# Four graph layers on one core: all start times of a planned instruction order laid out anew

## The chip, the cores and the metric

One core of one Trainium2 chip. The metric is the device time of one execution in microseconds (us), 64 graphs long.

## The reference, cut to what matters

64 graphs of 256 nodes with 512 features, float32. Each of four layers normalises the rows, applies relu, computes a graph layer and adds it to its input.

```python
def reference(x, adj, nodemask, ...):            # x 64x256x512, adj 64x256x256
    h = jnp.maximum(_layernorm(x, axis=-1), 0.0)
    x = x + _L0_gnn_ref(h, adj, ...)   # one softmax weight per node, times the values h @ Wv
    h = jnp.maximum(_layernorm(x, axis=-1), 0.0)
    x = x + _L1_gnn_ref(h, adj, ...)   # 8 heads of additive attention, masked by adj
    h = jnp.maximum(_layernorm(x, axis=-1), 0.0)
    x = x + _L2_gnn_ref(h, adj, ...)   # 8 heads, tanh(adj * scores)
    h = jnp.maximum(_layernorm(x, axis=-1), 0.0)
    x = x + _L3_gnn_ref(h, adj, nodemask, ...)   # as layer 0 with an adjacency aggregate
    return x
```

## The kernel before

A graph is some 150 named steps, each of which issues a few instructions on one engine. A table gives every step a time; the steps of all graphs are sorted by `graph * PERIOD + time`, and that sorted list is the order on each engine. No step waits for its time: the program takes only the order from the tables (a graph took 58.22 us in the trace that the prediction used, where `PERIOD` is 59.0). So the numbers of the tables are an order and nothing else. Some four to five graphs are in flight at once (by the plan 282.6 / 59).

```python
PERIOD = 59.0
TIMES = {
    "load": 0.000, "st0": 8.598, "at": 14.291, "rs0": 17.770, "pw0": 18.151, "sh0": 19.827, "hn0": 20.197,
    # ... some 140 more steps ...
    "softp3": 265.594, "pv31": 265.839, "softv3": 268.089, "softa3": 268.742, "pv30": 269.380, "softw3": 274.098,
    "add3": 280.909, "store": 282.605,
}
# ... WEIGHTS: the same for the set-up; FIRST: own tables of the first graphs; LAST: of the last ones ...

    def sequence(count):
        steps = [(at, -1, name) for name, at in WEIGHTS.items()]
        for b in range(count):
            times = FIRST[b] if b < len(FIRST) else LAST[b - count] if count - b <= len(LAST) else TIMES
            steps += [(b * PERIOD + at, b, name) for name, at in times.items()]
        return sorted(steps)
```

The steps that the argument touches, for a layer n: statistics `st`, variance plus epsilon `rs`, the power on GpSimd `pw`, the shift `sh`, relu on ScalarE `hn`, the 32x32 turn `sq`, the write of the turned squares to a scratch in DRAM `sw`, and the four reads that bring them back fully turned, `ht`. All transfers are issued through SyncE's queue (each line of the page's DMA issues is SPq), in the order of the sorted list.

```python
        @step("load")
        def _():
            nc.sync.dma_start(g.take("xt"), x[b].rearrange("(p c) d -> p c d", c=NC))           # 512 KB
            nc.sync.dma_start(g.take("adj", 4), adj[b].rearrange("(p c) m -> p c m", c=NC))     # 256 KB
            blocks = g.take("blocks")
            for q in range(4):                                                                  # 256 KB
                nc.sync.dma_start(blocks[q * S:(q + 1) * S],
                                  adj[b].rearrange("(a i) (q e) -> q i a e", i=S, q=4)[q])
# ...
            @step(f"pw{layer}")
            def _():
                nc.gpsimd.tensor_tensor(st["rstd"], st["rstd"], power, OP.pow)

            @step(f"sh{layer}")
            def _():
                st["shift"] = small.tile([P, NC], F32, name="shift")
                nc.vector.scalar_tensor_tensor(st["shift"], st["mv"][:, :, 0], -1.0, st["rstd"],
                                               op0=OP.mult, op1=OP.mult)
# ...
            @step(f"sw{layer}")
            def _():
                out_by_squares()               # one dma_start, 512 KB to the scratch

            @step(f"ht{layer}")
            def _():
                gathered(g.take("ht", users), st["sq_d"])   # four dma_start of 128 KB
```

TensorE steps: `qk`, `score0`, `pv` (values), `fa`/`fb` (features of layer 1), `po` and `su` (attention outputs and row sums), `xp` (projection), `xc` (C product), `ps`, `py` (layer 2 scores and outputs), `agg0`, `z` (layer 3).

## Time and profile before

| | |
|---|---|
| time, median of 3 runs | 3922.32 us (3916.96 to 3927.03) |
| medians of the rounds on the five chips used below | 3901 to 3916 us |
| TensorE busy | 94% of the span |
| span of the profiled execution the prediction used | 3892.8 us |

The profiled execution took 3894.62 us (its span, from the first to the last instruction, is 3892.8). The lines of the profile are in the prediction. There, the fences show in turn the page's busy times and slices, two windows, and the timelines of TensorE, VectorE and GpSimd.

### The profile page before, as it was taken

The numbers are of one execution on the slowest core, as the hardware profiler recorded it, in microseconds if no ns is written. First come the engines' busy times: TensorE is split into PE (matmuls) and PEld (weight loads), VectorE is DVE, ScalarE is ACT, GpSimd is POOL, SyncE is SP. The second block draws the span as 40 slices with busy tenths as digits, with TensorE's granted clock in tenths as the row PEclk, the third lists the DMA queues.
The fourth block names the chain that finished last, engine by engine and source line by source line (L and its number), as shares of the span: only waits on it lengthen the run. The fifth ranks groups of instructions, "written<-read, shape, count | busy, mean of one in ns | idle before, by whom it ended". The sixth has DMA issues, their size and how long they took to land.

```text
span 3892.8 us, 52870 instructions
## 1 busy us (share of the span) xinstructions
PE 3677.6 (94%) x16322; PEld 2126.0 (55%) x16322; DVE 3060.4 (79%) x7449; ACT 1872.2 (48%) x3653; POOL 1531.4 (39%) x1229
## 2 busy tenths in 40 slices
PE   6789999999999999999999999999999999999889
PEld 3455555555555555555555555555555555555544
DVE  5777787887888787787787787887788787787784
ACT  2444554545545544545544544545545544544442
POOL 1434343444344344343344344343344344344341
PEclk9899999999999999999999999999999999999999
DMA  7565666666666666666666666666666666666553
GB/s 200 168 193 179 208 200 212 214 203 213 216 201 211 217 200 212 207 199 207 215 195 213 207 202 214 214 204 209 216 201 216 214 198 215 209 200 196 181 182 103
DMA packets 967435, 784.71 MB, mean 202 GB/s; under 512 B 788913, under 2 KB 859121, under 8 KB 942577
## 3 DMA queue, kind: packets, MB, share of 16 engines
q1 hardware_dynamic: 967152, 781.34, 63.8%
q8 instruction: 130, 2.13, 0.2%
q14 instruction: 153, 1.25, 0.1%
HBM read 511.12 MB, written 270.01 MB: 201 GB/s over the span
## 4 chain that ended last, share of the span: by engine, by line
PE 46%; DVE 20%; DMA 17%; SPq 8%; issue 5%; POOL 3%; ACT 2%; DVEq 0%; ACTq 0%; POOLq 0%
PE bank L639 34%; DVE sq L645 7%; DMA ht<-sq_d 6%; SPq L650 5%; DMA sq_d<-sq 5%; PE bank L1111 4%; PE bank L966 3%; DVE pair L948 2%; DVE junk L896 2%; DMA hn<-sq_d 2%; PE bank L1097 2%; DVE stats L690 2%; DMA blocks<-in_adj_dram 2%; DVE xt L775 2%; DVE shift L706 1%
## 5 line engine op out<-in xcount | busy, mean ns | idle before, releaser
L639 PE MATMUL bank<-w_s,ht 128*128 128x256 f32 (+2 forms) x3072 | 965.7, 462 | 80.7 <-DMA ht<-sq_d 69.0
L639 PE MATMUL bank<-wv_s,ht 128*128 128x512 f32 x2048 | 906.3, 594 | 0.0
L639 PEld LDWEIGHTS bank<-w_s,ht 128*128 128x128 f32 x3072 | 587.4, 198 | 381.3 <-issue 288.2
L713 ACT ACTIVATE hn<-xt,shift,rstd 128x512 f32<-128x512 f32 x512 | 388.7, 806 | 828.8 <-DVE shift L706 759.5
L942 POOL TENSOR_TENSOR pair<-pair,negt 128x1024 f32<-128x1024 f32 x256 | 604.5, 2374 | 117.2 <-ACT pair L935 117.2
L639 PEld LDWEIGHTS bank<-wv_s,ht 128*128 128x128 f32 x2048 | 397.3, 197 | 444.8 <-issue 442.8
L975 POOL TENSOR_TENSOR half<-pair 128x512 f32<-128x512 f32 x256 | 331.3, 1306 | 593.1 <-PE bank L989 328.0
L896 DVE CUSTOM_DVE_ANT_0 junk<-all,adj 128x256 f32<-128x256 f32 x1024 | 472.8, 462 | 31.4 <-issue 0.2
L639 PE MATMUL bank<-m_s,ht 128*128 128x512 f32 x1024 | 455.5, 597 | 8.2 <-DMA ht<-sq_d 6.8
L935 ACT ACTIVATE pair<-all,ec 128x256 f32<-128x256 f32 x1024 | 433.4, 497 | 9.8 <-DMA all<-er_d 9.8
L1149 POOL TENSOR_TENSOR xt<-xt,hn 128x512 f32<-128x512 f32 x64 | 111.4, 1741 | 811.7 <-DMA hn<-sq_d 811.7
L690 DVE BATCH_NORM_STATS2 stats<-xt 128x6 f32<-128x512 f32 x512 | 332.3, 680 | 96.3 <-POOL xt L1034 88.5
L701 POOL TENSOR_TENSOR rstd<-rstd,power 128x2 f32<-128x2 f32 x256 | 179.5, 702 | 407.0 <-DVE rstd L697 390.9
L645 DVE STREAM_TRANSPOSE sq<-hn 128x512 f32<-128x512 f32 x512 | 331.8, 686 | 5.0 <-ACT hn L713 4.9
L966 PE MATMUL bank<-pair,feats 128*64 128x256 f32 x2048 | 272.4, 401 | 62.2 <-ACT pair L954 62.0
L1129 DVE TENSOR_TENSOR pair<-bank,at 128x512 f32<-128x512 f32 x512 | 317.0, 669 | 12.2 <-PE bank L1097 12.0
L954 ACT ACTIVATE pair<-pair 128x1024 f32<-128x1024 f32 x256 | 264.0, 1050 | 118.4 <-DVE pair L948 111.2
L639 PEld LDWEIGHTS bank<-m_s,ht 128*128 128x128 f32 x1024 | 197.2, 198 | 221.4 <-issue 216.4
L948 DVE TENSOR_TENSOR pair<-pair,all 128x1024 f32<-128x1024 f32 x256 | 303.4, 1223 | 15.3 <-DMA all<-m_d 14.4
L1032 POOL TENSOR_TENSOR hn<-hn,rs 128x256 f32<-128x256 f32 x256 | 152.3, 617 | 392.4 <-DMA hn<-sq_d 317.7
L761 ACT ACTIVATE bank<-bank,nmax 128x256 f32<-128x256 f32 x128 | 56.8, 443 | 504.5 <-DVE nmax L756 504.5
L1136 ACT ACTIVATE pair<-pair 128x512 f32<-128x512 f32 x512 | 285.8, 617 | 16.1 <-DVE pair L1129 16.0
(83 smaller groups left out, 4541.8 us busy)
## 6 DMA issues: line engine op xcount, KB each, us to landing
sq_d<-sq SPq DMA_DIRECT2D x448, 512.0 KB
ht<-sq_d SPq DMA_DIRECT2D x1024, 128.0 KB
all<-er_d SPq DMA_DIRECT2D x128, 1024.0 KB
all<-m_d SPq DMA_DIRECT2D x64, 1024.0 KB
hn<-sq_d SPq DMA_DIRECT2D x512, 128.0 KB
xt<-in_x_dram SPq DMA_DIRECT2D x64, 512.0 KB
xpt<-sq_d SPq DMA_DIRECT2D x256, 128.0 KB
out_dram<-xt SPq DMA_DIRECT2D x64, 512.0 KB
```

The lines of the kernel that those rows point to most:

```text
L639: nc.tensor.matmul(p, chunk(ht[:, k], c), w[:, k], start=(k == 0), stop=(k == KC - 1))
L645: nc.vector.transpose(sq.rearrange("p (r k i c) -> p c k r i", r=4, k=KC, c=NC)[:, c], t[:, c])
L690: nc.vector.bn_stats(stats[:, c, :], g["xt"][:, c, :])
L713: nc.scalar.activation(hn[:, c, :], g["xt"][:, c, :], AF.Relu, bias=st["shift"][:, c:c + 1], scale=st["rstd"][:, c:c + 1])
L896: nc.vector.tensor_tensor_reduce(junk, g["en"][:, h, :], g["adj"][:, c, :], 1.0, -BIG, OP.add, OP.max, g["mx"][:, c, h:h + 1])
L935: nc.scalar.activation(e[:, s, j, :], g["es"][:, h, :], AF.Prelu, bias=st["ec"][:, j, H + h:H + h + 1], alpha=0.2)
L942: nc.gpsimd.tensor_tensor(e, e, g["negt"][:, None].to_broadcast([P, 2, NC, N]), OP.add)
L948: nc.vector.tensor_tensor(e, e, g["m"][:, 2 * p:2 * p + 2, None, :].to_broadcast([P, 2, NC, N]), OP.subtract)
L966: nc.tensor.matmul(po[s * U:(s + 1) * U, p % 2, :], feats[:, j, h * U:(h + 1) * U], e[:, s, j, :], start=(j == 0), stop=(j == NC - 1))
L975: nc.gpsimd.tensor_tensor(g.take("half", name=f"h{p}"), e[:, :, 0, :], e[:, :, 1, :], OP.add)
L1129: nc.vector.tensor_tensor(th[:, s], g[f"ps{p}{s}"].rearrange("p (m n) -> p m n", m=NC), g["at"], OP.mult)
L1136: nc.scalar.activation(g[f"th{p}"][:, s], g[f"th{p}"][:, s], AF.Tanh)
```

## The change

Intent: a new plan with a shorter period (57 in place of 59) and no slack beyond the durations that a trace had shown. The instructions stay the same; every table (`TIMES`, `WEIGHTS`, six `FIRST` graphs, five `LAST` graphs) is replaced. The only other edit gives some set-up banks distinct names.

```diff
-PERIOD = 59.0
+PERIOD = 57.0
 TIMES = {
-    "load": 0.000, "st0": 8.598, "at": 14.291, "rs0": 17.770, "pw0": 18.151, "sh0": 19.827, "hn0": 20.197,
+    "load": 0.000, "at": 0.020, "st0": 0.021, "rs0": 0.040, "pw0": 0.060, "sh0": 0.447, "hn0": 0.467, "sq0": 4.046,
 ... (all of TIMES, WEIGHTS, FIRST and LAST likewise)
-    "add3": 280.909, "store": 282.605,
+    "pv31": 252.572, "softv3": 255.150, "softa3": 256.059, "softw3": 260.763, "add3": 262.405, "store": 266.901,
 }
@@ set-up
-                    pt = g.take("bank", name=f"wt{s}")
+                    pt = g.take("bank", name=f"wt{s}{e}")
 ... (and its three uses)
```

## The prediction

> **What bounds the kernel now.** I read the page first: which engine is full, at what clock.

> ```profile
> PE 3677.6 (94%) x16322; PEld 2126.0 (55%) x16322; DVE 3060.4 (79%) x7449; ACT 1872.2 (48%) x3653; POOL 1531.4 (39%) x1229
> ...
> PE   6789999999999999999999999999999999999889
> ...
> PEclk9899999999999999999999999999999999999999
> ```

> TensorE is busy 94% of the span, thin only in the first four and the last few slices, and its clock is full in between. The other engines have room. So a new order can give back only TensorE's idle time, and the next question is how much there is for one graph. The windows of 59 us (columns: stretch, length, then busy time and count for PE, PEld, DVE, ACT, POOL, then clock, DMA share and GB/s) show two paces in the middle:

> ```profile
> 767.00:826.00 59.00, 57.75 (x258) 33.40 (x257) 47.00 (x116) 30.36 (x61) 24.26 (x20) 1.00 0.65 207
> ...
> 1829.00:1888.00 59.00, 56.44 (x256) 32.84 (x255) 46.87 (x117) 29.45 (x59) 23.79 (x19) 1.00 0.66 207
> ```

> A graph is 254 matmul records, so 258 records in 59 us is a pace of about 58.1 us, and 256 one of 58.5. Over graphs 12 to 50 one and the same step returns every 58.24 us on average (57.3 to 59.9). The plan's own period was 59.0, so the chip beat it.

> Adding start-to-start times in the tensor timeline gives the floor for one graph: feature products 3.75 + 3.47, normaliser 0.23, z 6.97, the four value products 13.74, query/key 1.87, adjacency score 1.00, softmax broadcasts 0.54, projection 6.96, adjacency aggregate 3.43, C product 1.82, attention outputs 4.00, scores 3.88, their outputs 3.60, row sums 1.14: 56.40 us. The measured 58.24 therefore holds about 1.8 us of TensorE waits. The tensor timeline of one graph shows where they stand:

> ```profile
> 2011.32 3.68 PE L639 MATMUL bank<-w_s,ht 128*128 128x512 f32 x8 [0.89 <-DMA ht<-sq_d]
> ...
> 2036.40 1.08 PE L966 MATMUL bank<-pair,feats 128*64 128x256 f32 x8 [0.17 <-ACT pair L954]
> ...
> 2042.19 3.91 PE L639 MATMUL bank<-w_s,ht 128*128 128x272 f32 x16 [0.62 <-DMA ht<-sq_d]
> ```

> The bracket is the idle time before the group. Averaged over the middle graphs the three are 0.77 (projection, waits for its turned rows), 0.54 (third attention product, waits for the exponential) and 0.43 us (layer 1 features, wait for their turned rows): 1.74 of the 1.8. In the slow stretch the last one grows to 1.1 to 1.5 us, because issuing the four reads takes 3.1 us there in place of 2.55 and they land later.

> [...] The shift (L706, a 128x2 operation) and the GpSimd addition after the power:

> ```profile
> L706 DVE SCALAR_TENSOR_TENSOR shift<-mv,rstd x20: 147/154/2302, 2022.9 to 2292.3; 128x2 f32<-128x2 f32 x20
> ```
> ```profile
> 2028.31 0.70 POOL L701 TENSOR_TENSOR rstd<-rstd,power 128x2 f32<-128x2 f32 x1 [0.42 <-DVE rstd L697]
> 2028.97 2.35 POOL L942 TENSOR_TENSOR pair<-pair,negt 128x1024 f32<-128x1024 f32 x1
> ```
> ```profile
> 2029.04 2.30 DVE L706 SCALAR_TENSOR_TENSOR shift<-mv,rstd 128x2 f32<-128x2 f32 x1 [0.49 <-POOL rstd L701]
> ```

> The shift takes 0.15 us alone, and 2.30 when a 2.35 us GpSimd addition began just before; both end together. In all 48 middle graphs one of the four shifts pays this. [...] the trace has 2.6 us from issuing a scratch write to the first read behind it, then 2.55 us for issuing four reads and 2.1 (1.4 to 3.2) until the first features start.

> **The change, part by part.** Every table of times is replaced, the period goes from 59 to 57, and some setup banks get distinct names. No instruction is added or removed: counts on the engines are the same, so the floor stays 56.40. Only the order on each engine's queue and the buffers taken move. The new numbers cannot be read as start times (a 3.4 us value product stands 0.6 us before the next product), so I read them as order alone and lay one graph's round by hand with the old trace's durations. Zero is the end of the layer 0 value product pv00.

> What gets better: the projection's room. From the last attention product to xp0 lie 31.5 us of other matmuls in place of 28.8, so its 0.77 goes. The attention's first exponential is now early, behind only two matrix steps, so its 0.54 goes at that place. The features have 17.0 us behind pv00 in place of 16.0 behind pv01.

> What gets worse: VectorE's queue ahead of those features. The order is now score (L829), shift of layer 3, projection evictions, squares, softmax weight, one attention subtraction, and only then the layer 0 additions. Worked through:
> - adjacency score ends at -12.3; L829 to -11.5, transposed maxima and softmax weight to -10.75, statistics (1.49) to -9.25, variance and the power (0.70) to -8.25.
> - GpSimd then starts an addition (2.35) at once. The layer 3 shift comes at -7.6 and has to wait for its end: -5.85.
> - evictions and the negated maximum (0.42 + 0.68 + 0.39) to -4.35, turned squares to -3.0, second eviction to -2.35, projection squares (2.15) to -0.2, softmax weight to 0.3, attention subtraction (1.2) to 1.5.
> - layer 0 additions, which could start at 0.1, start at 1.5 and end at 2.85; statistics to 4.3, variance and power to 5.3.
> - the fourth GpSimd addition's input is ready at about 4.4, so it starts right behind the power and holds the shift by 2.35: 7.65. This is the same collision as in the lines above.
> - relu 1.52 to 9.25, turn to 10.45, write 2.85 to 13.3, issue of reads 2.65, landing 2.6: features at 18.55, against 17.0 of matmuls in front of them. TensorE waits 1.55.

> The wait would show in two pieces: about 1.3 us ahead of po0, whose exponential stands behind the relu and a copy on ScalarE (ends 11.05 where TensorE is at 9.7), the rest at the features. Sum: 56.40 + 1.55 = 57.95 us for a graph. The other way round the loop, from the features over the two broadcast reads, the four maxima and back to L829, comes to 27.2 us against 27.0 of matmuls, so it has hardly slack but adds nothing yet. I allow 0.1 us for landing scatter: 58.05, or 0.2 less than before. With some 52 graphs at full pace that is 10 us. The latency of a graph in the plan falls from 282.6 to 266.9 us, of which I credit 10 us to fill and drain together, my guess. 3922 - 20 = 3902 us.

> **The rivals.**
> 1. The plan is right: all three waits go, TensorE runs at its floor plus about 0.4 (56.8). 52 x 1.4 = 75 us and the same 10 at the ends: about 3837. For it: every matmul has more room on paper, and the old kernel ran faster than its plan. Against: the two collisions of a shift with a GpSimd addition, which follow from queue order.
> 2. The wait is replaced at full size or above: both loops through VectorE bind, and the slow read issue of the middle stretch adds 1.1 us throughout. Then a graph takes about 58.9, and the time is 3922 + 52 x 0.7 - 10 = about 3948. For it: the second loop has 0.2 us to spare at most, and a late GpSimd half-sum can hold an attention subtraction by 1.3 us.
> 3. The fill and drain decide. Before they cost about 165 us (3892.8 - 64 x 58.24) and their tables are new as well. Nothing in the trace tells how the new ones run; 20 us either way.

> **Range and chances.** The base is 3902. The pace is uncertain by 0.6 us for a graph (31 us), the ends by 20, together 37 as one deviation: 3852 to 3950 for 8 in 10. Faster by over 2% means under 3844, hence rival 1 nearly whole: 0.12. Slower by over 2%, over 4001, needs 59.7 us for a graph: 0.02. Within 2%: 0.86.

> **What will show it.** Right: a pace of 57.6 to 58.5 in the windows; a shift of 2.3 us still there, now with a second one of some 1.7 us for each graph; TensorE idle ahead of L966 behind ScalarE's pair or ahead of the 128x272 features, and little ahead of the 128x512 projection. Wrong: windows with 264 records and more (57.0 us or less for a graph), no long shifts, or fill slices that differ by more than 20 us. A pace of 59 with the idle time before L639 on ht reads would be rival 2.

## The result, and the profile after

The outputs are right. The changed kernel took 3876.72 us (median of 4 runs, 3874.68 to 3878.51), beside 3921.1 us for the kernel before in the same rounds. The ratio is 0.9886, 95% interval 0.9868 to 0.9903: the same by the measure of 2%, and 44 us less where 20 were forecast. A ratio here is the mean time of one kernel's runs over that of the other's of the same rounds, so not quite the ratio of the medians quoted. A later repeat on another chip gave 3862.13 beside 3900.92 us, ratio 0.9902 (0.9873 to 0.9932).

First the page of the changed kernel, the same three rows:

```profile
PE 3717.5 (96%) x16322; PEld 2105.0 (54%) x16322; DVE 3178.4 (82%) x7449; ACT 1893.0 (49%) x3653; POOL 1576.0 (41%) x1229
...
PE   7799999999999999999999999999999999999889
...
PEclk9899999999999999999999999999999999999999
```

The same 16322 matmul records are busy for 40 us more than in the profile of before (3717.5 against 3677.6), in a shorter span. That is the first surprise: the floor was not the same although no instruction was added. The first and the third slice are fuller (7 for 6, 9 for 8). The windows at the same places:

```profile
767.00:826.00 59.00, 57.70 (x257) 32.55 (x256) 49.88 (x118) 29.50 (x57) 24.91 (x20) 1.00 0.71 208
1829.00:1888.00 59.00, 56.09 (x253) 31.80 (x252) 48.47 (x115) 28.64 (x56) 24.16 (x19) 1.00 0.69 204
```

257 and 253 records in 59 us against 258 and 256 before: by its windows the middle is not faster than the profiled execution of before at all. Measured from one `pv00` to the next over graphs 12 to 50, a graph takes 58.64 us in this trace (58.28 in the repeat's). The kernel before had 58.22 in the trace that the prediction used, and 58.71 in a second one.

The timeline of TensorE through one graph (columns: start, length, engine, line, operation, output and inputs, count, and in brackets the idle time before it):

```profile
2018.02 1.08 PE L966 MATMUL bank<-pair,feats 128*64 128x256 f32 x8
2019.03 1.99 PE L1075 MATMUL bank<-xpt,c_s 128*128 128x256 f32 x8
2020.96 2.00 PE L966 MATMUL bank<-pair,feats 128*64 128x256 f32 x16
...
2026.07 3.91 PE L639 MATMUL bank<-w_s,ht 128*128 128x272 f32 x16 [0.61 <-DMA ht<-sq_d]
...
2032.76 3.60 PE L639 MATMUL bank<-m_s,ht 128*128 128x512 f32 x8
2036.29 1.95 PE L1111 MATMUL bank<-pair,xp 128*64 128x256 f32 x16
2038.17 0.43 PE L751 MATMUL bank<-ident,wc 128*128 128x128 f32 x2
2038.53 1.95 PE L1111 MATMUL bank<-pair,xp 128*64 128x256 f32 x16
2040.41 7.14 PE L639 MATMUL bank<-wv_s,ht 128*128 128x512 f32 x16
```

The waits ahead of the projection and of the third attention product are gone. One wait is left, ahead of the layer 1 features (128x272). Over graphs 12 to 49 it is 1.09 us, with 0.13 at `po0` and 0.03 at `z0`: 1.25 in all, where the second trace of before has 2.02 (0.92 at `xp0`, 0.56 at the features, 0.48 at `po2`, 0.05 at `z0`).

Now the floor. The same groups in the kernel before, in its second trace:

```profile
1506.17 1.89 PE L1075 MATMUL bank<-xpt,c_s 128*128 128x256 f32 x8
1507.99 1.95 PE L966 MATMUL bank<-pair,feats 128*64 128x256 f32 x16
...
1522.75 7.11 PE L639 MATMUL bank<-m_s,ht 128*128 128x512 f32 x16
1529.80 3.67 PE L1111 MATMUL bank<-pair,xp 128*64 128x256 f32 x32
1533.40 0.43 PE L751 MATMUL bank<-ident,wc 128*128 128x128 f32 x2
1533.67 7.04 PE L639 MATMUL bank<-wv_s,ht 128*128 128x512 f32 x16
```

Read start to start, since lengths overlap (the first group would end at 2019.10, the second starts at 2019.03). The C product (128\*128), which now stands between two half-width attention products (128\*64), takes 2020.96 - 2019.03 = 1.93 us, and 1507.99 - 1506.17 = 1.82 before. The layer 2 outputs (128\*64) were one run of 3.60 us; now a transpose splits them into 1.88 + 1.88, and the transpose itself takes 0.36 in place of 0.27. Half of `z` (`m_s`) with a full-size transpose in front of it (2032.76 to 2036.29) is still half of 7.05. So it is next to the changes between full-size and smaller matmuls that time is added: before has 4 such changes a graph, after has 12. The graph without its waits goes from 56.4 to about 57.2 us.

The collisions of the shift with GpSimd that the prediction worked out are there. All of the kernel's shifts (columns: minimum, median and maximum in ns behind the count), then their group on the page (count, busy us, mean ns, then idle before):

```profile
L706 DVE SCALAR_TENSOR_TENSOR shift<-mv,rstd x256: 108/162/2302, 7.3 to 3843.1; 128x2 f32<-128x2 f32 x128
```
```profile
L706 DVE SCALAR_TENSOR_TENSOR shift<-mv,rstd 128x2 f32<-128x2 f32 x256 | 257.2, 1005 | 47.1 <-POOL rstd L701 42.9
```

A mean of 1005 ns beside a median of 162: two of four shifts in each graph are held, layer 1's for 2.30 us and layer 3's for 1.88, in every one of the 38 middle graphs looked at. Of the 256 shifts in this trace 113 took over 1 us, and each of these ended within 0.03 us of the end of a GpSimd instruction that ran beside it. Attention subtractions (L948) are held as well: their median is 1.22 us, and 54 of 256, each with a half-sum of GpSimd (L975) beside it, took over 1.9.

Last, the beginning. Windows of 60 us while the pipeline fills, the second trace of before and then the changed kernel:

```profile
180.00:240.00 60.00, 49.78 (x206) 27.88 (x206) 42.62 (x86) 25.07 (x49) 24.95 (x18) 0.92 0.52 159
240.00:300.00 60.00, 55.69 (x257) 33.12 (x256) 45.97 (x129) 30.89 (x61) 18.92 (x16) 0.91 0.62 194
300.00:360.00 60.00, 55.55 (x230) 31.30 (x230) 49.35 (x94) 26.84 (x48) 27.34 (x23) 0.97 0.65 202
```
```profile
180.00:240.00 60.00, 56.24 (x250) 31.29 (x251) 54.74 (x128) 32.89 (x65) 29.07 (x21) 0.99 0.57 183
240.00:300.00 60.00, 58.89 (x257) 33.62 (x254) 48.39 (x119) 28.90 (x59) 27.30 (x21) 1.00 0.68 204
300.00:360.00 60.00, 59.78 (x262) 33.63 (x260) 49.81 (x114) 31.68 (x57) 27.90 (x22) 1.00 0.68 208
```

Here the kernels differ by far more than in the middle: TensorE reaches its full pace from 240 us on, at a clock of 0.99 to 1.00, where before ran at 0.91 to 0.97 with 4 to 10 us of idle time a window. The largest waits of TensorE from 180 to 360 us (total us, times, longest), again the second trace of before and then the changed kernel:

```profile
PE bank L966 <- ACT pair L954: 8.3, 3, 4.6
PE bank L639 <- DMA ht<-sq_d: 8.1, 6, 2.1
```
```profile
PE bank L639 <- DMA ht<-sq_d: 3.7, 2, 2.5
```

The waits of the attention products behind their exponential (L954) are gone, those for turned rows are half. Summing the nominal work of all TensorE steps done by a time and taking it from that time gives the time lost so far. At 420 us it is 128 us before and 109 after; from there to 3400 us 133 and 127; from there to the end 63.5 and 52. So in these two traces 19 of 36.5 us come from the fill, 11.5 from the drain and 6 from the long middle. One trace each is thin evidence for that, since a pace differs by 0.4 us between executions of one kernel; hence the experiments.

### The profile page after: what moved, and what is told of

Read it like the earlier page. It is cut to its first block, busy times and chain, and to the rows that moved or that the text cites.

```text
span 3876.7 us, 53433 instructions
## 1 busy us (share of the span) xinstructions
PE 3717.5 (96%) x16322; PEld 2105.0 (54%) x16322; DVE 3178.4 (82%) x7449; ACT 1893.0 (49%) x3653; POOL 1576.0 (41%) x1229
## 3 DMA queue, kind: packets, MB, share of 16 engines
q8 instruction: 131, 2.15, 0.2%
## 4 chain that ended last, share of the span: by engine, by line
PE 57%; DVE 14%; DMA 10%; issue 6%; SPq 6%; ACT 4%; POOL 3%; DVEq 0%; POOLq 0%; ACTq 0%
PE bank L639 39%; PE bank L1111 6%; SPq L650 5%; DMA ht<-sq_d 4%; DMA sq_d<-sq 4%; PE bank L1097 4%; DVE shift L706 3%; PE bank L966 3%; DVE sq L645 2%; DVE junk L896 2%; POOL pair L942 2%; ACT hn L713 2%; PE bank L1075 1%; DVE stats L690 1%; PE bank L821 1%
## 5 line engine op out<-in xcount | busy, mean ns | idle before, releaser
L639 PE MATMUL bank<-w_s,ht 128*128 128x256 f32 (+2 forms) x3072 | 964.2, 465 | 88.1 <-DMA ht<-sq_d 70.8
L639 PE MATMUL bank<-wv_s,ht 128*128 128x512 f32 x2048 | 919.5, 596 | 1.8 <-ACT qk L811 1.7
L639 PEld LDWEIGHTS bank<-w_s,ht 128*128 128x128 f32 x3072 | 598.6, 200 | 407.5 <-issue 263.7
L942 POOL TENSOR_TENSOR pair<-pair,negt 128x1024 f32<-128x1024 f32 x256 | 607.3, 2384 | 121.5 <-ACT pair L935 121.5
L639 PEld LDWEIGHTS bank<-wv_s,ht 128*128 128x128 f32 x2048 | 392.2, 196 | 440.5 <-issue 436.6
L975 POOL TENSOR_TENSOR half<-pair 128x512 f32<-128x512 f32 x256 | 388.8, 1531 | 325.5 <-ACT pair L954 198.3
L701 POOL TENSOR_TENSOR rstd<-rstd,power 128x2 f32<-128x2 f32 x256 | 179.6, 702 | 787.8 <-DVE rstd L697 786.8
L896 DVE CUSTOM_DVE_ANT_0 junk<-all,adj 128x256 f32<-128x256 f32 x1024 | 460.5, 450 | 31.0
L639 PE MATMUL bank<-m_s,ht 128*128 128x512 f32 x1024 | 466.8, 599 | 5.3 <-DMA ht<-sq_d 3.9
L954 ACT ACTIVATE pair<-pair 128x1024 f32<-128x1024 f32 x256 | 269.7, 1057 | 327.6 <-DVE pair L948 326.9
L948 DVE TENSOR_TENSOR pair<-pair,all 128x1024 f32<-128x1024 f32 x256 | 365.9, 1451 | 3.0 <-DMA all<-m_d 2.8
L1149 POOL TENSOR_TENSOR xt<-xt,hn 128x512 f32<-128x512 f32 x64 | 90.7, 1417 | 653.7 <-DMA hn<-sq_d 653.7
L1136 ACT ACTIVATE pair<-pair 128x512 f32<-128x512 f32 x512 | 295.2, 626 | 74.8 <-DVE pair L1129 74.8
L639 PEld LDWEIGHTS bank<-m_s,ht 128*128 128x128 f32 x1024 | 192.5, 197 | 213.9 <-issue 211.2
L966 PE MATMUL bank<-pair,feats 128*64 128x256 f32 x2048 | 271.8, 399 | 25.5 <-ACT pair L954 19.0
L706 DVE SCALAR_TENSOR_TENSOR shift<-mv,rstd 128x2 f32<-128x2 f32 x256 | 257.2, 1005 | 47.1 <-POOL rstd L701 42.9
```

Source lines behind the costliest of these rows:

```text
L639: nc.tensor.matmul(p, chunk(ht[:, k], c), w[:, k], start=(k == 0), stop=(k == KC - 1))
L896: nc.vector.tensor_tensor_reduce(junk, g["en"][:, h, :], g["adj"][:, c, :], 1.0, -BIG, OP.add, OP.max, g["mx"][:, c, h:h + 1])
L942: nc.gpsimd.tensor_tensor(e, e, g["negt"][:, None].to_broadcast([P, 2, NC, N]), OP.add)
L948: nc.vector.tensor_tensor(e, e, g["m"][:, 2 * p:2 * p + 2, None, :].to_broadcast([P, 2, NC, N]), OP.subtract)
L966: nc.tensor.matmul(po[s * U:(s + 1) * U, p % 2, :], feats[:, j, h * U:(h + 1) * U], e[:, s, j, :], start=(j == 0), stop=(j == NC - 1))
L975: nc.gpsimd.tensor_tensor(g.take("half", name=f"h{p}"), e[:, :, 0, :], e[:, :, 1, :], OP.add)
```

## The experiments

The theory I began with: the changed middle is held by the wait at the features, made by the held shift of layer 1; TensorE's floor rose by its changes of matmul size; the ends made the rest. The rival: something in the DMA queue makes that wait.

### First round: the shift and TensorE's order

The kernel before once more, on the chip of this round, to see whether its first trace was typical.

> The kernel before, unchanged, for a second trace on the chip of the other runs. Its first trace was 27 us shorter than its timed runs (3894.6 against 3917 to 3927), while the changed kernel's trace is as long as its timed runs. Theory A (the first trace was a lucky run): this trace spans 3915 to 3925 us, and the extra 25 us are wider waits in the middle stretch, so a pace near 58.7 us for a graph over graphs 12 to 50 in place of 58.22. Theory B (fill and drain differ from run to run): the pace stays 58.2 and the extra time lies before graph 12 or after graph 50.

3915.26 us (3912.01 to 3915.78), ratio 1.0011 (0.9994 to 1.0028); pace 58.71 in its trace. So the first trace, at 58.22, was a fast one, and a pace read from it was half a microsecond too low.

The shift of layer 1 on ScalarE, with the mean negated in place (one small VectorE instruction more a graph):

```diff
+                if layer in (1,):                       # in step rs
+                    nc.vector.tensor_scalar(st["mv"][:, :, 0], st["mv"][:, :, 0], -1.0, None, op0=OP.mult)
                 st["shift"] = small.tile([P, NC], F32, name="shift")
-                nc.vector.scalar_tensor_tensor(...)
+                if layer in (1,):                       # in step sh
+                    for c in range(NC):
+                        nc.scalar.activation(st["shift"][:, c:c + 1], st["mv"][:, c, 0:1], AF.Identity,
+                                             scale=st["rstd"][:, c:c + 1])
+                else:
+                    nc.vector.scalar_tensor_tensor(...)
```

> The changed kernel with one part altered: the layer 1 shift is computed on ScalarE (two 128x1 activations) from a negated mean, so VectorE's small shift no longer waits 2.3 us for the GpSimd addition. Theory of the held shift: features are ready about 1.7 us earlier, TensorE's wait ahead of the features (1.1 us for a graph) shrinks under 0.2, pace 57.3 to 57.6 in place of 58.6, time 50 to 65 us under the changed kernel (about 3815 to 3830). Rival (the read issue and its landing set the wait, whatever the shift does): the wait stays over 0.8 us and the time within 10 us of 3877.

3892.62 us (3890.48 to 3898.88), ratio 0.9957 (0.9938 to 0.9976). Not faster than the changed kernel. The held shift did go: the turn `sq1` ended 7.25 us after the end of `pv00`, not 9.26. But the write `sw1` started only at 8.57 and the reads `ht1` were issued at 13.36 us, as in the changed kernel (13.33). The 2.0 us won on VectorE vanished in the DMA queue. My theory of the wait fell here, or so it looked.

Three TensorE steps moved so that equal sizes stand together:

```diff
-    "po2": 107.965   "xc": 167.559   "z0": 223.305   "softp3": 243.288
+    "po2": 108.000   "xc": 164.000   "z0": 219.500   "softp3": 244.750
```

> The changed kernel with three steps moved on TensorE alone, so that matmuls of 64 rows or columns stand together: the layer 3 broadcast behind the second output product, z0 and the C product ahead of the first attention product. Six of twelve changes between full and half-size matmuls in a graph go. Theory of the dearer changes (each costs about 0.1 us): TensorE busy falls by 0.5 to 0.6 us a graph (total 3717 to about 3690), but most of it turns into a longer wait ahead of the features, because that wait hangs on the VectorE chain; pace 58.3 to 58.5, time 5 to 15 us under 3877. Rival (matmul cost does not depend on neighbours, the higher busy time is an artefact of modelled ends): busy stays 3717 within 8 us.

3870.07 us (3862.97 to 3880.05), ratio 0.9898 (0.987 to 0.9926). TensorE was busy 3680.2 us, 37 less than in the changed kernel with the same instructions (27 were expected), and a graph without its waits is back at 56.5 us. So the order alone made the floor's rise, and three steps hold nearly all of it. Per change the cost is not one number: six changes fewer took 0.8 us out, the two that remain above before's four cost under 0.1. In time it bought little: the pace is 58.24 us, and much of the time won as work became waits. Another part went late in the run, where these tables meet the unaltered `LAST` tables: from `pv00` of graph 55 to the end this trace takes 654.7 us, the changed kernel's two 642.4 and 641.6.

Both edits:

> Both of the two edits before together. If the held shift sets the wait and the changes set the floor, both gains now show: pace 56.7 to 57.0, TensorE busy about 3690, time 85 to 100 us under 3877 (about 3780 to 3795). If only the shift matters: about 3820. If neither: 3870 or more.

3883.24 us (3874.16 to 3886.88), ratio 0.9927 (0.9906 to 0.9948). Nothing added. What the queue does comes next.

### Second round: the ends transplanted, and the load moved

The middle of before with the beginning of the changed kernel, then with both ends (tables exchanged, and 2 and 5 steps at the seams moved later so that nothing runs ahead of what it needs).

> Before's middle and before's end, with the changed kernel's beginning (its first six graphs' times and its places for the weights; 2 steps at the seam moved later so that nothing runs ahead of what it needs). Theory A, the ends carry most of the gain: time less the work of the matmuls, summed to 420 us, stood at 128 us in the unchanged kernel run again and at 109 us in the changed one, so this kernel should show about 109 to 112 there and end about 17 to 19 us earlier than before, a ratio of about 0.995 to 0.996, with the pace of the middle at before's 58.2 to 58.7 us. Theory B, the middle carries it: the ratio is 0.999 to 1.001 and the beginning's gain is given back at the seam or soon after it.

> Before's middle with both of the changed kernel's ends (first six and last five graphs). Theory A: the drain's gain of about 11 us (time after the last middle graph's pv00: 948.9 us in before run again, 935.4 in the changed kernel) adds to the fill's 19, so about 30 us less than before, a ratio of about 0.992, at an unchanged pace of the middle; that would be some two thirds to three quarters of the whole change. Theory B: the ends are worth little, the ratio is 0.998 or above.

3947.38 us (ratio 1.012, 1.01 to 1.014) and 3998.44 us (1.0244, 1.0229 to 1.0259): both slower than before, against both theories. The transplanted beginning works as in its own kernel up to 360 us, where 105 us are lost (126 before, 99 after). Then the two plans do not mesh at the seam. The waits of TensorE there (total us, times, longest), in the first transplant from 420 to 600 us:

```profile
PE bank L521 <- DMA ht<-sq_d: 33.5, 2, 21.9
PE bank L521 <- DVE mx L778: 4.7, 1, 4.7
```

Two waits alone cost 33.5 us. These ends could not be tried under the other plan's middle, so the two runs say nothing on how the whole gain is split. A better test is in the third round.

In the changed kernel the load of a later graph stands right in front of the write `sw1` in the queue. The timeline of SyncE's queue (the `sq_d<-sq` of 2017.36 is `sw1`, the `ht<-sq_d` of 2021.03 are its reads):

```profile
2013.42 0.62 SPq L661 DMA_DIRECT2D xt<-in_x_dram  x1
2014.08 0.43 SPq L662 DMA_DIRECT2D adj<-in_adj_dram  x1
2014.56 1.91 SPq L666 DMA_DIRECT2D blocks<-in_adj_dram  x4
2017.36 0.34 SPq L733 DMA_DIRECT2D sq_d<-sq  x1
2021.03 2.56 SPq L650 DMA_DIRECT2D ht<-sq_d  x4
```

From the end of the write's issue to the reads' issue pass 3.33 us here, 3.63 in the median. Where nothing is close in front of it, as ahead of `swo` or `sw2`, the same kernel needs 2.5 to 2.7. Why the load holds the reads up is not shown: the runs below move it, and none of them separates its place in the order from the load merely keeping the DMA engines busy.

The load moved 13 us earlier, in front of the reads `xpt`:

```diff
+            early = 13.15 if 8 <= b < count - len(LAST) else 0.0
-            steps += [(b * PERIOD + at, b, name) ...]
+            steps += [(b * PERIOD + at - (early if name == "load" else 0.0), b, name) ...]
```

> The changed kernel with one thing moved: the loads of the middle graphs (features, adjacency, blocks) are issued 13 us earlier in the order of the DMA queue, between the read ht3 and the read xpt, and no longer right in front of the scratch write sw1. Theory A, the load in front of the write makes the wait at the features: from sw1's end on the engine to the issue of the read ht1 falls from 4.0 us (median) to about 2.8, as before has it, the wait ahead of fa0 falls from about 1.1 us a graph to 0.0 to 0.3, the pace from 58.64 to 57.6 to 57.9 us, and the time by 35 to 50 us against the changed kernel (3826 to 3842 beside 3876). Theory B, the held shift of layer 1 on VectorE makes it: write to issue may shorten, but fa0 still waits 0.8 us or more, and the time is within 10 us of the changed kernel's.

3876.5 us (3866.9 to 3878.98), ratio 0.9927 (0.9909 to 0.9945). The waits of TensorE from 800 to 2900 us, the changed kernel and then this one:

```profile
PE bank L639 <- DMA ht<-sq_d: 30.6, 22, 2.8
PE bank L639 <- DVE sq L645: 8.0, 8, 1.4
```
```profile
PE bank L1076 <- DMA xpt<-sq_d: 33.9, 34, 1.9
PE bank L640 <- DMA ht<-sq_d: 4.7, 6, 1.3
```

The wait at the features is nearly gone and as large a one stands ahead of the C product, whose reads are now behind the load. Write to issue fell only to 3.34; those later reads now stand in front of the write. Neither theory was met whole: the wait was exchanged, not removed.

> The same, with the three TensorE steps moved as in the run r_group (softp3 after py1, z0 and xc earlier). If the load's move takes out the wait at the features, the shorter work of TensorE shows in full: pace 56.8 to 57.3 us, PE busy about 3680 us, time about 3800 to 3825. If the wait stays, the time is within 10 us of r_group's 3870.

4022.86 us (4000.44 to 4027.43), ratio 1.0295 (1.0263 to 1.0327). The C product stands 3.6 us earlier on TensorE here, and its wait rose to 101.4 us in 33 waits in the same stretch. In addition most graphs ran at a mean clock of 0.972; see below.

### Third round: both kernels cut short, and the load taken apart

Each kernel with 24 graphs in place of 64, with its own ends; wrong, since 40 outputs stay unwritten:

```diff
-    plan.run(weights, graph, B)
+    plan.run(weights, graph, 24)
```

> The kernel before, cut to its first 24 graphs (the outputs of the other 40 stay unwritten, so it is wrong on purpose; its beginning and its end are those of the full kernel). With 40 graphs fewer at the pace of 58.71 us read from the trace of before run again, the time falls by 2348 us, to about 1565 us where before takes about 3913. This run and the next divide each kernel's time, with no trace needed, into a pace (the time of 64 graphs less that of 24, over 40) and the two ends (what remains).

> The changed kernel cut to 24 graphs in the same way. Theory A, the gain lies in the fill and the drain: it takes 27 to 37 us less than the cut kernel before (about 1533 us), nearly the whole gain of the 64 graphs, and the pace of the 40 graphs taken out is the same in both within 0.2 us. Theory B, the gain lies in the middle: the cut kernels differ by a third of the full gain (12 to 15 us), and the paces by about 0.6 us.

1562.15 us (1559.88 to 1568.82) for before and 1535.98 (1530.18 to 1539.92) for the changed kernel, beside 3915.18 us for the full kernel before. So 26.2 us of the gain are there with 24 graphs. For the full changed kernel on this chip I take 3915.18 times the two measured ratios, 3871 to 3877 us, hence a full gain of 38 to 45 us. The 40 graphs taken out then gain (38.4 - 26.2) / 40 = 0.31 to (44.6 - 26.2) / 40 = 0.46 us each; before's pace is (3915.18 - 1562.15) / 40 = 58.83 us. The cut kernels still hold 13 middle graphs (24 less 6 and 5), so the ends alone are worth 26.2 - 13 x 0.31 to 0.46, which is 20 to 22 us, and the full middle of 53 graphs 16 to 24. But these times are not known that well. The difference of the cut kernels has a standard error of 2.6 us over its nine runs, and the ends of the two ratios' intervals put the full gain anywhere from 27 to 52 us, so the gain of a middle graph is not clear of zero here.

The traces kept of these runs settle the split better. Take the time up to the start of `pv00` of graph 11, and from the start of `pv00` of the sixth graph from the end (58 of 64, 18 of 24) to the end of the span, with TensorE's idle time in each:

| trace | up to graph 11, us | idle | last stretch, us | idle |
|---|---|---|---|---|
| before, as used in the prediction | 677.5 | 88.8 | 478.7 | 43.7 |
| before, second trace | 675.7 | 88.0 | 481.2 | 46.8 |
| before, 24 graphs | 676.1 | 89.7 | 479.5 | 42.7 |
| changed | 654.7 | 67.8 | 467.7 | 32.9 |
| changed, the repeat of the fourth round | 653.5 | 65.0 | 466.5 | 32.0 |
| changed, 24 graphs | 651.3 | 66.7 | 465.6 | 32.0 |

Three traces of a kernel agree within 3.5 us, and the kernels differ by 23 us in the fill and 13 in the drain: 36 us for both ends (30 to 37 with the boundaries set elsewhere, from graph 6 to 14). TensorE's idle time falls by as much, 22 and 12 us. What lies between, graphs 11 to 58 of the full kernels, took 2736.6 and 2756.3 us before and 2754.3 and 2737.7 us changed, so the kernels do not differ there beyond the 20 us between two executions of one. The 20 to 22 us above came out too small because they credit each middle graph of the cut kernels with a gain; in their traces the seven graphs from 11 to 18 took 404.8 us before and 411.5 changed. So theory A holds: about 36 of the 38 to 44 us lie in the ends, and what is left for the middle is not clear of zero.

The load taken apart, first attempt: adjacency and blocks behind `ht2`, the features behind the store.

```diff
-            nc.sync.dma_start(g.take("adj", 4), ...)     # and blocks, in step "load"
+        @step("loada")                                    # a step of their own
@@ in sequence(), graphs 11 to 58
+                times.update(load=-18.0, loada=-25.0)
```

> The changed kernel with the load taken apart, for graphs 11 to 58: the adjacency and the blocks are issued 25 us before their present place, after the read ht2, where the DMA queue stood idle, and the features 18 us before it, behind the store, where it stood idle too. So neither the write sw1 nor the read xpt has a load right in front of it. The run e_load had only exchanged one wait for the other: from fa0 (0.85 us a graph taken out) to xc (0.85 us put in). Theory A, what stands right in front of a write or a read in the queue sets the wait: the write sw1 to the issue of ht1 falls from 4.0 to about 2.8 us, the waits ahead of fa0 and xc are both under 0.3 us a graph, pace 57.5 to 57.8 us, time 3830 to 3850 us. Theory B, a chain of one length through VectorE and the queue closes anyhow and the wait turns up at another step (z0, xp0, fa0): pace 58.3 to 58.7 us, time 3860 to 3880.

> The same with the three TensorE steps moved as in r_group. Theory A: PE busy about 3680 us, pace 57.0 to 57.4 us, time 3805 to 3835 us, faster than the changed kernel by 1 to 2 per cent. Theory B: time within 10 us of r_group's 3870, or slower where xc, which stands 3.6 us earlier on TensorE, waits for its read as in the run e_load_group (2.5 to 4 us a graph).

4026.22 us (ratio 1.0286, 1.0272 to 1.03) and 4057.86 us (1.0363, 1.0349 to 1.0377). The queue's own waits from 800 to 2900 us, and the clock:

```profile
SPq L664 <- DMA out_dram<-xt: 204.0, 34, 7.3
```
```profile
core 0: 4033.1 us, clock 0.969
```

| TensorE idle within one window of 3.41 us | windows | next window at half clock |
|---|---|---|
| under 1.8 us | 11589 | 19 |
| 1.8 to 2.0 us | 18 | 10 |
| 2.0 us and more | 124 | 124 |

Of the 19 in the first row, 15 stand right behind a window that was itself at half clock after one of the last row. So what counted was whether 2 us of a wait fell into one window. In the whole trace of the changed kernel 14 waits of TensorE last 2.0 to 3.2 us: 7 put 2.05 us or more into one window and half clock followed each time, and 7 are cut by the grid into parts of at most 1.76 us, and it followed none of them.

### Fourth round: the load taken apart without the store

Adjacency and blocks alone go behind `ht2`; the features stay.

```diff
-                times.update(load=-18.0, loada=-25.0)
+                times["loada"] = -30.5
```

> The changed kernel with the adjacency and the blocks (512 KB of a graph's 1 MB load, five of its six transfers) issued after the read ht2, where the run e_split showed them to fit without delaying the next write; the features stay where the changed kernel has them, so that no load waits for the store, which cost e_split 5.7 us a graph. Theory A, what stands right in front of the write sw1 sets the wait at fa0: the queue reaches sw1 with 3 us to spare after the features' issue, write to issue of ht1 2.4 to 3.0 us instead of 3.6, fa0's wait 0.0 to 0.4 us a graph instead of 1.1, no wait above 2 us (so no half-clock stretches), pace 57.5 to 57.9 us, time 3830 to 3855. Theory B, the wait turns up elsewhere: pace 58.3 to 58.7, time 3865 to 3885.

> The same with the three TensorE steps moved as in r_group: theory A pace 57.0 to 57.4 us, PE busy about 3680, time 3805 to 3835. Theory B within 10 us of r_group's 3870. If xp0's read, which has the adjacency and the blocks right behind it (slack fell from 3.3 to 0.4 us in e_split), becomes late, the wait is seen ahead of xp0.

> The same with the shift of layer 1 on ScalarE too. If the queue had hidden the gain of 0.76 us that the run r_act showed at sq1, it must show now: fa0's wait 0.0 us, pace 0.0 to 0.4 us below that of e_adj_group. If the held shift does not matter, the time equals e_adj_group's or is up to 10 us longer, as r_both's was than r_group's.

> The changed kernel unaltered, on the same chip and beside the same runs of before as the three above: 3876 us within 0.3 per cent, ratio 0.988 to 0.991.

| run | time, us | ratio (interval) | pace in the trace, us | waits of TensorE a graph, us |
|---|---|---|---|---|
| changed kernel again | 3862.13 | 0.9902 (0.9873 to 0.9932) | 58.28 | 0.99 |
| load apart | 3828.38 | 0.981 (0.9786 to 0.9834) | 57.47 | 0.24 |
| and TensorE's order | 3831.53 | 0.9814 (0.9788 to 0.9841) | 57.22 | 0.78 |
| and the shift | 3800.07 | 0.9733 (0.9705 to 0.9761) | 56.62 | 0.36 |

Moving half of the load takes 34 us off the changed kernel. The queue around the write (here the write is at 2048.30 and its reads at 2050.95), and what is left of the waits from 800 to 2900 us:

```profile
2044.33 0.62 SPq L664 DMA_DIRECT2D xt<-in_x_dram  x1
2048.30 0.33 SPq L739 DMA_DIRECT2D sq_d<-sq  x1
2050.95 2.54 SPq L653 DMA_DIRECT2D ht<-sq_d  x4
```
```profile
PE bank L642 <- DMA ht<-sq_d: 2.5, 5, 0.6
PE bank L972 <- ACT pair L960: 1.5, 4, 0.5
```

Write to issue 2.32 us in place of 3.33, with nothing issued in the 3.35 us before the write. Everything before the write is unchanged: in the median `sq1` ends 9.27 us after `pv00`'s end (9.26 in the changed kernel) and the write is issued at 9.29 in both, with layer 1's shift still held for 2.30 us in all 38 graphs. Only the reads come earlier, at 11.98 instead of 13.33. That is the clean separation: the load ahead of the write made the wait at the features, theory A, with the held shift in place. Most graphs now last 57.34 us, the work of the order alone and the 0.13 at `po0`.

The third row met no theory: TensorE's busy time fell to 3672.4 us, but the time did not. Many graphs in a row last 57.0 us with small waits at `po3`, behind an exponential (13.3 us in 25 waits from 800 to 2900 us) that waits for VectorE (189.2 us in 110 waits for all of L960), and at `z0`. With the shift on ScalarE as well (fourth row) the wait at `po3` goes, most of that at `z0` stays (0.23 of 0.26 us), and the time is 31 us less. There the shift counts. Of the 0.6 us a graph 0.4 are waits; the other 0.2 is a smaller floor (56.44 to 56.26 us), which no run explains.

### Fifth round: the missing corner, and the other shift

> The changed kernel with adjacency and blocks issued after ht2 and the shift of layer 1 on ScalarE, TensorE's order as in the changed kernel: the fourth corner beside e_adj, e_adj_group and e_adj_both. In e_adj nearly every graph lasts 57.34 us, which is TensorE's own work of 57.21 and the 0.13 at po0; the held shift costs nothing there any more. Theory A, each of the three (load in front of the write, switches of TensorE, held shift) counts only once the ones that hide it are gone: this run is within 10 us of e_adj's 3828, pace 57.2 to 57.5. Theory B, the shift's edit is worth 0.6 us a graph by itself, as between e_adj_group and e_adj_both: pace 56.8 to 56.9, time 3795 to 3805.

> e_adj_both with the shift of layer 3 on ScalarE as well. Pace of e_adj_both 56.62 us, of which about 0.4 are waits left at z0, fa0 and xc and 56.2 TensorE's own work. The shift of layer 3 lies on the way to z0 (layer 3's scratch write and read), so theory A: z0's wait shrinks and the pace falls to 56.2 to 56.5, time 3780 to 3800, at most 20 us less than e_adj_both. Theory B, z0's wait comes from what stands in the DMA queue: no difference beyond 8 us.

Load apart and the shift, TensorE's order left: 3818.09 us (3813.03 to 3821.86), ratio 0.9748 (0.9729 to 0.9768), on another chip, where before took 3916.09. Pace 57.27 us; most graphs last 57.09 with no wait at all. By pace it lies where theory A put it, by time at the edge (10.3 us under the load apart alone); by the ratio it is 0.6% better than the load apart alone, nearer to theory B. I leave its worth at 10 to 24 us. Either way there is a gain that the same edit did not have while the load stood before the write (ratio 0.9957 against the changed kernel's 0.9886).

Both shifts on ScalarE: 3808.05 us (3802.53 to 3811.71), ratio 0.9726 (0.9705 to 0.9748). No different from one shift, as theory B had it: the rest of the wait at `z0` does not come from the held shift of layer 3.

The load apart, the order and the shift together thus beat both kernels: 2.7% under before, and 1.6% under the changed kernel on the same chip (3800.07 and 3862.13).

## Why the prediction was wrong

It forecast 20 us and 44 came (38 in the repeat). The half of the sum that it guessed, the ends, holds the whole error; the half that it worked out holds several errors that cancel.

- **The ends.** The step that failed was "I credit 10 us to fill and drain together, my guess". By six traces they are worth about 36: 23 in the fill, 13 in the drain, as idle time of TensorE that went. It is the term of the sum that was mis-sized, by some 26 us. The prediction itself said that nothing in the trace tells how the new end tables run, and still put a number on them; its own sign of being wrong, fill slices that differ by more than 20 us, came. In the fill most of the gain is in waits between 180 and 360 us, 19 to 23 us before and 4 to 5 after. Which of the moved steps does it stays open, since the transplant failed at its seam.
- **The middle's size.** "58.05, or 0.2 less than before. With some 52 graphs at full pace that is 10 us": the runs neither show this nor rule it out. Both sides were too low. The pace of before was read as 58.24 from one execution that was 0.7% faster than the timed ones; the second trace has 58.71, and the timed difference of 64 and 24 graphs 58.83. On the right side 58.28 to 58.64 came. That the two errors cancel in the difference is luck.
- **"So the floor stays 56.40"** was wrong by 0.8 us a graph. The instructions are the same, but their neighbours are not: 12 changes of matmul size a graph against 4. Moving three steps back together took 37 us of busy time out.
- **The waits.** It forecast 1.55 us, of which about 1.3 at `po0` and the rest at the features; 1.0 to 1.25 came, nearly all at the features and 0.13 at `po0`. The relu that the exponential of `po0` stands behind ended at 8.47 us, not at 9.25, so TensorE, there at 9.8, hardly had to wait. That the waits at the projection and at the third attention product would go was right.
- **The held shifts** came as forecast: 2.30 us for layer 1 (2.35 in the sum) and, new, 1.88 for layer 3 (1.75). But "write 2.85 to 13.3" hid two errors. The reads were issued at 13.33 as forecast, because the write began 1.2 us earlier than worked out (9.29 for 10.45) and took 1.2 us longer (4.0 for 2.85). A number that comes out right in the middle of a chain does not prove its links. The write took longer with the load right ahead of it in the new order (2.3 us in place of 3.6 once half of the load was moved), which no step of the prediction looked at.
- **Rival 3**, the ends deciding with 20 us either way, was the nearest of the three; rival 2's slower pace of 58.9 and rival 1's floor did not come.

## What to carry to other kernels

When a change moves order alone, count three things besides the waits: the neighbours of each matmul (here 12 changes of size a graph in place of 4 went with 40 us more of TensorE time), what stands in front of each write in the DMA queue (here 2.3 us from write to reads in place of 3.6), and whether the trace's execution is as long as the timed ones (here it was 0.7% shorter). A cause on one engine can be real and worth nothing until the cause hiding it is gone (here the shift's edit made the changed kernel no faster, and took 10 to 31 us off once half of the load was moved), so try edits together before dropping one. To split a gain between ends and middle, compare the time to one inner iteration and from another to the end in several traces; two timed lengths alone need the middle to run at one pace, which it did not here. Mark a guess in a sum as the term to be measured first: here it held the error.
